# A four-layer graph network on one core: layer 1's norm from accumulated row sums and ScalarE squares

## The chip, the core and the metric

The kernel runs on one core of one Trainium2 chip. A core has TensorE (PE; its weight loads are listed as PEld), VectorE (DVE), ScalarE (ACT), GpSimd (POOL) and SyncE (SP, which here only starts DMAs). The metric is the device time of one execution in microseconds.

## The reference

Sixteen graphs ("batches") of 1024 nodes with 256 features pass through four layers. Each layer normalises its input over the features, applies relu, runs a graph operation with the adjacency matrix, and adds the result to its input. Layers 0 and 1, where the change lies:

```python
# layernorm: (x - mean) / sqrt(var + 1e-5), over the last axis
h = jnp.maximum(_layernorm(x), 0.0)
x = x + L0(h, adj)        # attention-like weights: a = u / sum(u), u = mask * exp(e + f)
h = jnp.maximum(_layernorm(x), 0.0)
x = x + L1(h, adj)        # d^-1/2 adj d^-1/2 @ (h @ weight) + bias
```

Layer 2 is a recurrence over the nodes, layer 3 a product with the adjacency matrix and a two-layer network. Both read what layers 0 and 1 have left in DRAM.

## The kernel before

A batch's x is held in SBUF as 8 tiles of 128 nodes x 256 features. `layers_0_1` fixes the order of the instructions of all five engines by hand: each engine runs its queue in program order, so an instruction that waits holds up everything behind it on that engine.

For each batch i the loop does an "a half" (layer 0) and a "d half" (layer 1). Each half forms its product with the adjacency matrix in `sums`, as seven block products on quarters of the matrix (`b11`, `b21`, `t1` to `t4`, `b22`), into the PSUM banks px, py and pz. The sums and differences of quarters (`add_halves`, L620) and of activations (`combos`: `s1`, `s2`, then two more) are made by VectorE. Between the block products the code calls hooks (`a0` to `a6`, `d0` to `d6`), which put other work into the engines' queues: loads, the next batch's statistics, and `side(...)`, which gives VectorE pieces of the ordering work that layer 2 needs.

After the a half, `weights` multiplies the result by layer 0's matrix `w0`: TensorE makes two tiles at a time into one of three `pmm` buffers (L418), and VectorE adds each tile, scaled, to x (L421). Layer 1's norm needs the mean and variance of these new rows. Before the change the `then` argument calls `stats` after each tile, so VectorE runs bn_stats (L323) and bn_aggr (L324) for it. Then `inv_sqrt` lets VectorE scale and POOL raise to the power -1/2 (L82, L86), VectorE forms `rd` and `shift` (L712, L714), and ScalarE's `normed` writes relu((x - mean) * scale) into `h1` (L353), which the first product of the d half reads. While that goes on, TensorE runs the product with `w1` of the *previous* batch (`second_weights`: two pairs before, two pairs behind the place where `run_a.turn` stands). Batch 0 has no previous batch.

The *next* batch's statistics for layer 0 are made by ScalarE, in the class `Moments`: `first` sums the rows (L337), `middle` lets VectorE form the negative mean (L340), `second` sums the squares of x minus the mean (L345), `root` makes the power. Their unneeded elementwise output goes to a scrap tile of PSUM, named `pt`, of which there are two buffers. `second(lo)` for the first four tiles stands in hook `a6`, `second(hi)` for the other four between `sums` and `weights`.

From batch 9 on the loop also prepares two batches per turn for layer 2, as `Job`s. `run_a.turn()` transposes a batch on TensorE into the same two `pt` buffers, in four groups (L535), and ScalarE copies each group out (L538); `run_a.rest()` (`first`, `order`, `base`) follows after the second `w1` pairs, and ends with stores issued by POOL. Batches 14 and 15 are prepared after the loop, where x[15] also gets its `w1` product and its norm.

At the very start VectorE copies the vector `v` out of PSUM (L603), a product of TensorE (L309) that needs loaded weights, then makes the statistics of batch 0 (`stats`), then the sums `add_f` (L437) that lead over `end_f` (L443) to the products of `degrees` (L459).

Of the kernel before, what the change touches and what calls it, by code (L numbers as in the profile page):

```python
# [9 lines left out]
F32 = mybir.dt.float32  # L10
AF = mybir.ActivationFunctionType
ALU = mybir.AluOpType
# [4 lines left out]
P = 128  # L17
B, N, D, H = 16, 1024, 256, 1024
NT = N // P
# [12 lines left out]
LN_EPS = 1e-5  # L32
# [4 lines left out]
def bcast_row(ap, n):  # L37

    return bass.AP(tensor=ap.tensor, offset=ap.offset, ap=[[0, P], [1, n]])
# [3 lines left out]
def gnn_stack(ctx: ExitStack, tc: tile.TileContext, a: dict, out: bass.AP):  # L43
    nc = tc.nc
# [30 lines left out]
    def rows(ap):  # L75
        return ap.rearrange("(t p) d -> p t d", p=P)

    def inv_sqrt(pool, src, eps, shape, name, mul=1.0):

        t = pool.tile(shape, F32, name=name + "_v")  # L80
        if mul == 1.0:
            nc.vector.tensor_scalar(t, src, eps, None, op0=ALU.add)  # L82
        else:
            nc.vector.tensor_scalar(t, src, mul, eps, op0=ALU.mult, op1=ALU.add)
        r = pool.tile(shape, F32, name=name)
        nc.gpsimd.tensor_tensor(r, t, mhalf.to_broadcast(shape), ALU.pow)  # L86
# [177 lines left out]
    def layers_0_1():  # L264
        with ExitStack() as st:
# [54 lines left out]
            def stats(x, tiles, mv):  # L320
                for t in tiles:
                    s6 = small.tile([P, 6], F32, name="s6", bufs=4)
                    nc.vector.bn_stats(s6, x[:, t])  # L323
                    nc.vector.bn_aggr(mv[:, t], s6)  # L324

            class Moments:


                def __init__(self, x):
                    self.x = x  # L330
                    self.ssq, self.neg = (small.tile([P, NT], F32, name=n) for n in ("m_ssq", "m_neg"))
                    self.sum = small.tile([P, NT], F32, name="m_sum", bufs=1)

                def first(self, tiles):
                    junk = psum.tile([P, 512], F32, name="pt")[:, :D]
# [4 lines left out]
                    nc.vector.tensor_scalar(self.neg, self.sum, -1.0 / D, None, op0=ALU.mult)  # L340

                def second(self, tiles):
                    junk = psum.tile([P, 512], F32, name="pt")[:, :D]
                    for t in tiles:
                        nc.scalar.activation(junk, self.x[:, t], AF.Square, bias=self.neg[:, t : t + 1],  # L345
                                             accum_out=self.ssq[:, t : t + 1])

                def root(self):
                    self.rs = inv_sqrt(small, self.ssq, LN_EPS, [P, NT], "rs", mul=1.0 / D)

            def normed(h, x, shift, scale, tiles):
                for t in tiles:
                    nc.scalar.activation(h[:, t], x[:, t], AF.Relu, bias=shift[:, t : t + 1], scale=scale[:, t : t + 1])  # L353
# [56 lines left out]
                hooks[6]()  # L410
                return ag

            def weights(x, ag, w, scale, then=lambda t: None, pairs=range(0, NT, 2)):
                for t0 in pairs:
                    po = psum.tile([P, 2, D], F32, name="pmm", bufs=3)
                    for t in (t0, t0 + 1):
                        for c in range(DC):
                            nc.tensor.matmul(po[:, t - t0], ag[:, c, t * P : (t + 1) * P], w[:, c],  # L418
                                             start=c == 0, stop=c == DC - 1)
                    for t in (t0, t0 + 1):  # L420
                        nc.vector.scalar_tensor_tensor(x[:, t], po[:, t - t0], scale[:, t : t + 1], x[:, t],  # L421
                                                       op0=ALU.mult, op1=ALU.add)
                        then(t)

            def begin_f(b, tiles):
                m = mean[b]
# [173 lines left out]
            all_ = range(NT)  # L600
            lo, hi = range(NT // 2), range(NT // 2, NT)

            nc.vector.tensor_copy(v, pv)  # L603
            mean[0] = m = Moments(x[0])
            mv = small.tile([P, NT, 2], F32, name="mv")
            stats(x[0], all_, mv)
            m.neg = small.tile([P, NT], F32, name="m_neg")
            nc.vector.tensor_scalar(m.neg, mv[:, :, 0], -1.0, None, op0=ALU.mult)
            m.rs = inv_sqrt(small, mv[:, :, 1], LN_EPS, [P, NT], "rs")
            nc.sync.dma_start(vec["W_b"], bcast_row(a["W_b"], D))  # L610
            nc.sync.dma_start(w0, a["W_wT"].rearrange("(c p) e -> p c e", p=P))
            begin_f(0, all_)
# [26 lines left out]
            for i in range(B):  # L639
                run_a, run_b = jobs.get(i, (None, None))  # L640
                here, ahead, behind = i < B, i + 1 < B, i > 0
                got = {}
# [7 lines left out]
                def a1():  # L650
                    if ahead:
                        get(i + 1, "b11", 0, 0)
                    second()
                    add_halves(i, "t4", "t2", "b21")
# [50 lines left out]
                pairs = list(range(0, NT, 2))  # L705
                second_weights(pairs[:2])
                pairs = pairs[2:]
                if run_a:
                    run_a.turn()
                if here:  # L710
                    rd = small.tile([P, NT], F32, name="rd")
                    nc.vector.tensor_mul(rd, rs, dis[i])  # L712
                    shift = small.tile([P, NT], F32, name="shift")
                    nc.vector.scalar_tensor_tensor(shift, mv[:, :, 0], -1.0, rd, op0=ALU.mult, op1=ALU.mult)  # L714
                    h1[i] = big.tile([P, NT, D], F32, name="h1")
                    normed(h1[i], x[i], shift, rd, all_)
                    if ahead:
                        mean[i + 1].root()
# [10 lines left out]
                m2 = Moments(x[i - 1]) if behind else None  # L729
# [80 lines left out]
            mv = small.tile([P, NT, 2], F32, name="mv")  # L810
# [6 lines left out]
            nc.vector.scalar_tensor_tensor(shift, mv[:, :, 0], -1.0, rs, op0=ALU.mult, op1=ALU.mult)  # L817
# [5 lines left out]
            normed(h2[15], x[15], shift, rs, all_)  # L823
            nc.sync.dma_start(rows(he_d[15]), h2[15])
            job15.load()
            job14.first()
# [596 lines left out]
    def layer_3(shared, x, hn, at, h, eye):  # L1423
        with ExitStack() as st:
# [274 lines left out]
            for b in range(B):  # L1699
# [91 lines left out]
```

## Time and profile before

| what | value |
|---|---|
| median of 3 runs | 4239.55 us (4235.62 to 4241.14) |
| the profiled execution | 4237.46 us, span in the profile 4235.8 us |
| busy, share of the span | PE 95%, DVE 63%, POOL 39%, ACT 37% |
| layers 0 and 1 | about the first 1340 us of the span |
| DMA, mean over the span | 176 GB/s |

The profile is one execution on the chip. For each engine it gives the instructions with start and duration, and for each idle stretch the instruction that ended it (written `<-`). A row of a timeline holds the start in us, the duration or, for merged rows, the stretch in us, the engine, the line of the kernel, the operation, the output and the inputs, and in brackets the idle time before it with its releaser. A matmul in f32 appears as two instructions. The granted TensorE clock is given as a share of full speed.

### The profile page before, as it was taken

How to read it: one execution, taken by the hardware profiler on the slowest of the kernel's cores; microseconds unless marked ns; L12 is line 12 of the kernel's file. 1: busy time of each engine (PE TensorE's matmuls, PEld its weight loads, DVE VectorE, ACT ScalarE, POOL GpSimd, SP SyncE). 2: the span in 40 equal slices, each digit the busy share in tenths (PEclk: the TensorE clock that was granted, in tenths of full speed). 3: DMA queues.
4: the chain of work that ended last, by engine and by line, in shares of the span. 5: the costliest groups of instructions: out<-in, count | busy, mean ns of one | idle time of the engine just before them, and what ended most of it. 6: DMA issues, size and time to landing. Idle time of an engine off the chain costs nothing. (4 is left out here: it accounts for less than half of the span.)

```text
span 4235.8 us, 56395 instructions
## 1 busy us (share of the span) xinstructions
PE 4031.0 (95%) x19307; PEld 2803.9 (66%) x19307; DVE 2676.5 (63%) x6286; ACT 1552.3 (37%) x3900; POOL 1644.6 (39%) x1740
## 2 busy tenths in 40 slices
PE   7999999999997999999999999998899999999998
PEld 3545455555555888888888888877365665756656
DVE  7889887478873445444444444453577777777776
ACT  3454545444433232322323232323333334333332
POOL 2132323443434323243333333332546355464552
PEclk9999999999998999999999999998899999999999
DMA  6667666988858454646454645431533434434320
GB/s 234 213 219 238 201 216 232 282 283 290 307 190 267 142 180 155 194 136 200 136 190 148 195 155 180 140 113 36 206 127 130 169 118 142 139 120 171 118 100 20
DMA packets 406701, 744.72 MB, mean 176 GB/s; under 512 B 75168, under 2 KB 325664, under 8 KB 365344
## 3 DMA queue, kind: packets, MB, share of 16 engines
q1 hardware_dynamic: 370976, 613.49, 42.3%
q0 software_dynamic: 26080, 109.21, 9.1%
q10 hardware_dynamic: 9216, 16.78, 1.1%
q8 instruction: 210, 3.44, 0.3%
q14 instruction: 219, 1.79, 0.1%
HBM read 538.85 MB, written 183.76 MB: 171 GB/s over the span
## 5 line engine op out<-in xcount | busy, mean ns | idle before, releaser
L86 POOL TENSOR_TENSOR rs<-rs_v,mhalf 128x8 f32<-128x8 f32 (+1 forms) x65 | 112.2, 1727 | 931.8 <-DVE rs_v L82 720.5
L928 PE MATMUL pf<-hb,ab 128*128 128x256 f32 x1568 | 415.2, 383 | 0.0
L1041 PE MATMUL pf<-hs,wx 128*128 128x256 f32 x1536 | 348.0, 383 | 11.6 <-POOL hs L1032 11.4
L1041 PEld LDWEIGHTS pf<-hs,wx 128*128 128x128 f32 x1536 | 293.7, 192 | 55.0 <-POOL hs L1032 12.6
L1569 POOL TENSOR_TENSOR ss<-ss,sq 128x512 f32<-128x512 f32 x224 | 299.0, 1350 | 24.5 <-ACT sq L1567 18.5
L1341 POOL DMA_INDIRECT hs_d<-h,table x128 | 128.9, 1007 | 461.4 <-ACT gates L1049 401.7
L928 PEld LDWEIGHTS pf<-hb,ab 128*128 128x128 f32 x1568 | 272.1, 191 | 37.3 <-issue 6.7
L1046 DVE TENSOR_TENSOR gates<-pf,bias 128x512 f32<-128x512 f32 x128 | 88.4, 691 | 285.3 <-PE pf L1041 285.2
L418 PE MATMUL pmm<-w,ag 128*128 128x256 f32 x1024 | 242.6, 391 | 27.0 <-DVE x L421 13.8
L1632 PEld LDWEIGHTS po<-w,hh 128*128 128x128 f32 x2048 | 238.2, 193 | 16.6 <-issue 11.0
L418 PEld LDWEIGHTS pmm<-w,ag 128*128 128x128 f32 x1024 | 194.8, 194 | 77.2 <-DVE x L421 31.2
L1632 PE MATMUL po<-w,hh 128*128 128x128 f32 x2048 | 242.4, 277 | 1.4 <-ACT hh L1615 0.7
L1567 ACT ACTIVATE sq<-hh 128x512 f32<-128x512 f32 x224 | 141.2, 630 | 198.0 <-POOL ss L1569 113.8
L1515 PE MATMUL ph<-bxt,hb 128*128 128x512 f32 x440 | 199.5, 599 | 3.3 <-ACT hb L1487 1.9
L1139 ACT ACTIVATE r<-pr 128x128 f32<-128x128 f32 (+2 forms) x256 | 57.8, 278 | 361.6 <-PE pr L1095 356.6
L1077 PE MATMUL pf<-bd,h 128*128 128x384 f32 (+4 forms) x512 | 184.6, 450 | 0.8 <-DVE bxt L1080 0.8
L1080 DVE TENSOR_TENSOR bxt<-bxt,pf 128x384 f32<-128x384 f32 (+4 forms) x256 | 127.7, 500 | 82.0 <-PE pf L1077 79.6
L1565 DVE SCALAR_TENSOR_TENSOR hh<-ph,b,u 128x512 f32<-128x512 f32 x192 | 141.2, 749 | 47.2 <-PE ph L1561 37.4
L1615 ACT ACTIVATE hh<-hh,rw 128x512 f32<-128x512 f32 x256 | 158.7, 709 | 23.7 <-DVE hh L1614 23.7
L1614 DVE TENSOR_TENSOR hh<-hh,po 128x512 f32<-128x512 f32 x256 | 154.3, 673 | 2.9 <-PE po L1611 2.9
L345 ACT ACTIVATE pt<-x,m_neg 128x256 f32<-128x256 f32 x240 | 114.3, 476 | 107.8 <-DVE m_neg L340 101.5
L1515 PEld LDWEIGHTS ph<-bxt,hb 128*128 128x128 f32 x440 | 82.8, 192 | 101.2 <-issue 93.7
(363 smaller groups left out, 9225.9 us busy)
## 6 DMA issues: line engine op xcount, KB each, us to landing
at<-in_quarters SPq DMA_DIRECT2D x94, 1024.0 KB, 9.9
t_d<-at SPq DMA_DIRECT2D x64, 1024.0 KB, 11.5
ab<-in_columns SPq DMA_DIRECT2D x127, 512.0 KB, 5.0
bxt<-t_d SPq DMA_DIRECT2D x42, 1024.0 KB, 4.8
bxt<-in_quarters SPq DMA_DIRECT2D x34, 1024.0 KB, 4.8
at<-at POOLq DMA_DIRECT2D x30, 1024.0 KB, 10.8
at<-t_d SPq DMA_DIRECT2D x22, 1024.0 KB, 6.2
pc<-in_own ACTq DMA_DIRECT2D x64, 256.0 KB, 7.2
```

What stands on the lines that cost most here:

```text
L418: nc.tensor.matmul(po[:, t - t0], ag[:, c, t * P : (t + 1) * P], w[:, c], start=c == 0, stop=c == DC - 1)
L928: nc.tensor.matmul(pb, ab[:, jts[k]], hb[:, jts[k]], start=k == 0, stop=k == len(jts) - 1)
L1041: nc.tensor.matmul(pg[:, e], wx[:, c, q * D + e * P : q * D + (e + 1) * P], self.hs[:, c], start=c == 0, stop=c == DC - 1)
L1077: nc.tensor.matmul(pf, h[:, g, c * P : (c + 1) * P], bd[:, g, b0 : b0 + n, S : S + far], start=True, stop=True)
L1341: nc.gpsimd.indirect_dma_start(out=hs_d[t][g][:, :], out_offset=row(1, g, t, s), in_=h[:, g], in_offset=None)
L1515: nc.tensor.matmul(pa, st[left][:, k], at[q % 6][:, k], start=onto is None and k == 0, stop=k == 3, skip_group_check=True)
L1565: behind3[:] = [nc.vector.scalar_tensor_tensor(hh[q][:, k], ph, b1[:, k : k + 1], u, op0=ALU.add, op1=ALU.add)]
L1567: nc.scalar.activation(sq, hh[q][:, k], AF.Square)
L1569: nc.gpsimd.tensor_tensor(ss[q], ss[q], sq, ALU.add)
L1614: nc.vector.tensor_mul(hh[q][:, k], hh[q][:, k], pr)
L1615: nc.scalar.activation(hh[q][:, k], hh[q][:, k], AF.Silu, scale=rw[:, k : k + 1])
L1632: nc.tensor.matmul(po[:, n], left[:, c, n * P : (n + 1) * P], right[:, c], start=onto is None and n == 0 and c == 0, stop=c == HH - 1, ski ...
```

## The change

`weights` no longer calls `stats`. With `norm` given, each of VectorE's additions also delivers the sum of the new row (`accum_out`). After each pair of tiles `pair` lets VectorE form the two negative means and puts two squares with accumulation into ScalarE's queue; their elementwise output goes to the first tile of `h1`, which is allocated earlier for this. `root` then makes the power. The next batch's `second(hi)` now comes after `weights` and `root`. The same is done for x[15] after the loop, with `s2` as scrap. At the start, v's copy moves behind the statistics of batch 0.

```diff
+                def pair(self, t):
+                    two = slice(t, t + 2)
+                    nc.vector.tensor_scalar(self.neg[:, two], self.sum[:, two], -1.0 / D, None, op0=ALU.mult)
+                    self.second((t, t + 1))
...
-            def weights(x, ag, w, scale, then=lambda t: None, pairs=range(0, NT, 2)):
+            def weights(x, ag, w, scale, norm=None, pairs=range(0, NT, 2)):
...
+                        more = {"accum_out": norm.sum[:, t : t + 1]} if norm else {}
                         nc.vector.scalar_tensor_tensor(x[:, t], po[:, t - t0], scale[:, t : t + 1], x[:, t],
-                                                       op0=ALU.mult, op1=ALU.add)
-                        then(t)
+                                                       op0=ALU.mult, op1=ALU.add, **more)
+                    if norm:
+                        norm.pair(t0)
...
-            nc.vector.tensor_copy(v, pv)
             mean[0] = m = Moments(x[0])
...
             m.rs = inv_sqrt(small, mv[:, :, 1], LN_EPS, [P, NT], "rs")
+            nc.vector.tensor_copy(v, pv)
...
-                    mv = small.tile([P, NT, 2], F32, name="mv")
+                    h1[i] = big.tile([P, NT, D], F32, name="h1")
+                    m1 = Moments(x[i], "n", h1[i][:, 0])
+                    weights(x[i], ag, w0, got["rc"], m1)
+                    m1.root()
                     if ahead:
                         mean[i + 1].second(hi)
-                    weights(x[i], ag, w0, got["rc"], lambda t: stats(x[i], (t,), mv))
-                    rs = inv_sqrt(small, mv[:, :, 1], LN_EPS, [P, NT], "rs")
...
-                    nc.vector.tensor_mul(rd, rs, dis[i])
+                    nc.vector.tensor_mul(rd, m1.rs, dis[i])
                     shift = small.tile([P, NT], F32, name="shift")
-                    nc.vector.scalar_tensor_tensor(shift, mv[:, :, 0], -1.0, rd, op0=ALU.mult, op1=ALU.mult)
-                    h1[i] = big.tile([P, NT, D], F32, name="h1")
+                    nc.vector.tensor_mul(shift, m1.neg, rd)
...
-            weights(x[15], ags[15], w1, dis[15], lambda t: stats(x[15], (t,), mv))
+            m2 = Moments(x[15], "n", big.tile([P, 2, D], F32, name="s2").rearrange("p a d -> p (a d)")[:, :D])
+            weights(x[15], ags[15], w1, dis[15], m2)
             nc.sync.dma_start(rows(x2_d[15]), x[15])
-            rs = inv_sqrt(small, mv[:, :, 1], LN_EPS, [P, NT], "rs")
+            m2.root()
```

More of the change, by code (lines that the diff above doesn't have):

```diff
@@ L326, in layers_0_1, with __init__ @@
             class Moments:
[L329 to L332, printed above, removed]
+                def __init__(self, x, name="m", junk=None):
+                    self.x, self.junk = x, junk
+                    self.ssq, self.neg = (small.tile([P, NT], F32, name=name + n) for n in ("_ssq", "_neg"))
+                    self.sum = small.tile([P, NT], F32, name=name + "_sum", bufs=1)
                 def first(self, tiles):
@@ L342, in second @@
                 def second(self, tiles):
-                    junk = psum.tile([P, 512], F32, name="pt")[:, :D]
+                    junk = self.junk if self.junk is not None else psum.tile([P, 512], F32, name="pt")[:, :D]
                     for t in tiles:
@@ L809, in layers_0_1 @@
             job14.load()
-            mv = small.tile([P, NT, 2], F32, name="mv")
-            weights(x[15], ags[15], w1, dis[15], lambda t: stats(x[15], (t,), mv))
+            m2 = Moments(x[15], "n", big.tile([P, 2, D], F32, name="s2").rearrange("p a d -> p (a d)")[:, :D])
+            weights(x[15], ags[15], w1, dis[15], m2)
             nc.sync.dma_start(rows(x2_d[15]), x[15])
-            rs = inv_sqrt(small, mv[:, :, 1], LN_EPS, [P, NT], "rs")
+            m2.root()
             run_b.first()
@@ L816, in layers_0_1 @@
             shift = small.tile([P, NT], F32, name="shift")
-            nc.vector.scalar_tensor_tensor(shift, mv[:, :, 0], -1.0, rs, op0=ALU.mult, op1=ALU.mult)
+            nc.vector.tensor_mul(shift, m2.neg, m2.rs)
             job14.mask()
@@ L822, in layers_0_1 @@
             h2[15] = big.tile([P, NT, D], F32, name="h2", bufs=2)
-            normed(h2[15], x[15], shift, rs, all_)
+            normed(h2[15], x[15], shift, m2.rs, all_)
             nc.sync.dma_start(rows(he_d[15]), h2[15])
```

## The prediction

> **What bounds the kernel now.** I read the page's engine totals first, then TensorE's waits in the first 1340 us (layers 0 and 1), then the timelines of one vector-bound batch and one batch with layer 2's preparation.
>
> ```profile
> PE 4031.0 (95%) x19307; PEld 2803.9 (66%) x19307; DVE 2676.5 (63%) x6286; ACT 1552.3 (37%) x3900; POOL 1644.6 (39%) x1740
> ```
>
> TensorE is busy for 95% of the span, so an edit on another engine pays only where TensorE waits. Its waits (total us, times, longest):
>
> ```profile
> PE pmm L418 <- DVE x L421: 13.8, 8, 2.9
> PE pt L459 <- ACT gs L443: 12.3, 1, 12.3
> ...
> PE pt L558 <- ACT hT L565: 8.2, 6, 4.0
> ...
> PE px L382 <- ACT h L353: 8.0, 1, 8.0
> ```
>
> The change touches three of these: the weight product waiting for the vector's additions (L418), the start (L459), and batch 0's wait for layer 1's norm (L382). Everything it can gain lies there. Batch 1, vector then TensorE:
>
> ```profile
> 131.89 0.48 DVE L421 SCALAR_TENSOR_TENSOR x<-pmm,rc,x 128x256 f32<-128x256 f32 x1
> 132.40 0.43 DVE L323 BATCH_NORM_STATS2 s<-x 128x6 f32<-128x256 f32 x1
> 132.86 0.18 DVE L324 BATCH_NORM_AGGREGATE mv<-s 128x2 f32<-128x6 f32 x1
> 132.96 0.45 DVE L421 SCALAR_TENSOR_TENSOR x<-pmm,rc,x 128x256 f32<-128x256 f32 x1
> ```
> ```profile
> 133.46 10.59 PE L418 MATMUL pmm<-w,ag 128*128 128x256 f32 x40 [2.04 <-DVE x L421]
> 143.89 3.60 PE L382 MATMUL px<-at,h 128*128 128x512 f32 x8
> ```
>
> A tile costs the vector 1.06 us (131.89 to 132.96), a pair 2.1, while TensorE makes a pair in 1.72 (13.7 us for eight, from batches that flow). With three pmm buffers TensorE falls to the vector's pace.
>
> Batch 11, where `turn` stands between the weight products, ScalarE and TensorE:
>
> ```profile
> 890.82 1.07 ACT L538 COPY hT<-pt 128x512 f32<-128x512 f32 x2 [6.26 <-issue]
> ```
> ```profile
> 890.14 1.04 PE L535 MATMUL pt<-to,h 128*128 128x128 f32 x8
> 891.46 1.15 PE L535 MATMUL pt<-to,h 128*128 128x128 f32 x8 [0.28 <-ACT hT L538]
> 892.44 3.62 PE L418 MATMUL pmm<-w,ag 128*128 128x256 f32 x16
> ```
>
> ScalarE had been idle for 6.26 us when the transposes came, so its copies followed at once. That idle time is what the change fills.
>
> [...] TensorE's waits of 3.48 us (batch 13), but also of 2.75, 2.08 and 2.04 us (batches 14, 12, 1) are followed by a granted 0.50; waits of 1.94, 2.84, 2.88 and 2.95 us are not. Batch 13's stage (busy time of PE, PEld, DVE, ACT and POOL, then the granted clock, DMA share, GB/s):
>
> ```profile
> 1070.00:1072.00 2.00, 2.00 (x5) 1.64 (x6) 1.82 (x9) 1.90 (x7) 0.00 (x0) 0.50 1.00 422
> ```
>
> [...] the trace shows no overtaking, and my loss rests on this. [...] The trace agrees, on L437, and gives the price:
>
> ```profile
> 511.49 0.48 DVE L437 SCALAR_TENSOR_TENSOR pt<-q,rs,v 128x256 f32<-128x256 f32 x1
> 511.89 0.14 DVE L437 DVE_READ_ACCUMULATOR pt<-q,rs,v 128x1 f32 x1
> 512.14 0.49 DVE L437 SCALAR_TENSOR_TENSOR pt<-q,rs,v 128x256 f32<-128x256 f32 x1
> ```
>
> **The change, part by part.** L421 with an accumulator is not in the trace; L437 has the same form and repeats every 0.655 us. `pair` adds a 128x2 scaling, about 0.08. So a pair costs the vector 1.39 us (bounds: 1.3 with the scaling hidden, 1.6 if the read waits for the write), against 2.1. ScalarE gets eight squares a batch at 0.632 each (L345's rhythm), 5.06 us, and in its queue they stand *ahead of* the second half of the next batch's squares (four, 2.53 us).
>
> Call the vector's first addition t0. Vector-bound, the last scaling starts at t0 + 5.5; ScalarE follows 0.2 later and ends its last two squares at t0 + 7.0, the next batch's half at H = t0 + 9.53. The vector stands still from 5.6 to 7.15 because `root` waits for ScalarE; behind it wait the four additions of the previous batch's w1 product, so TensorE's last pair starts at t0 + 8.15, just about when it would anyway. From rs_v to ScalarE's first `normed` the trace has 2.45 us (140.44 to 142.89), hence t0 + 9.6, and TensorE's px at t0 + 10.25.
>
> *Batches 1 to 8.* t0 is set by ordering work ahead of it, which stays. Batch 1: t0 = 131.89, px 142.14 against 143.89: 1.75. Batches 2 to 5: t0 + 11.66 now, so 1.4 each, 5.6. Batch 6 has only 0.67 us over its 13.7 to give: 0.65. Batches 7 and 8: 1.3 each. Sum 10.6; less 0.7 because batch 1's half clock (from 134.85) may now bind: **-9.9**.
>
> *Batch 0.* No w1 product fills the wait; px at t0 + 11.59 becomes t0 + 10.25: **-1.4**. TensorE still idles some 6.7 us, so the cold product behind it (5.94 us instead of 3.6) stays.
>
> *The start.* Statistics need only x. The SP queue's waits before its quarter loads place x's last pair at about 6.95 us; eight tiles at 0.525 then end at about 8.0, the power at 10.1, and v's copy (its product ends at 10.10) is done at 10.5. The sums of L437 start at 10.6 instead of 16.87, `degrees` at 16.1 instead of 22.39: 6.3 earlier. Quarters b11, b21 and t3 have landed by 12.21, 14.66 and 17.06 (what the SP queue waits for); b22, by that step, at 19.5, when it is needed. Late next is t1, due at about 22 by the same 2.4 us step: L620's additions, 22.46 before, start at 22.0. They were hidden; now their chain to s2 (10.26 us, 22.46 to 32.72) ends at 32.2, TensorE has waited since 28.1, and it starts that product at 32.3 instead of 34.44, half-clocked after a 4 us wait (about 2 us back). Bounds: nothing, and 4 us if t1 lands at 20.5 and the clock holds. I take **-1**.
>
> *Batches 9 to 14.* `turn` stands behind all those squares in ScalarE's queue. Its second transpose group needs the pt buffer that the next batch's last squares use as scrap, and its copies come behind them. So the group starts at H + 0.1 and the last pairs of w1 at H + 1.9 (copy 0.57, transposes 0.5, twice) = t0 + 11.4. Before it was t0 + 9.93 in batches 9, 11 and 13: +1.5 each. Batch 10 flows at TensorE's pace (H = 783.48 + 12.6): +1.8, of which about 1.4 counts, since `order` then waits for the heT_d store, which is issued later too. Batch 12 was late already: +0.6; batch 14, half-clocked through its w0 pairs: +1.7. With 1.58 for batch 9 the sum is **+8.3**; `order`, `first` and the d half follow unshortened. Batch 15 has no next batch: 0. The turn's wait (T(A) ends at t0 + 7.0, the next group starts at 9.6) is 2.6 us, in the length where four of eight throttled: three times 1.8 us, **+5.4** (bounds 0 and 11).
>
> *The end.* x[15]'s squares queue behind h2[14]'s norm (to 1310.6) and end at 1315.7; bs and run_b's copies behind them were at 1314.88. Everything to the last he_d store and job15's load follows: **+0.8**.
>
> What leaves the vector (8 x 0.4 us a batch) is worth nothing beyond this: its queue empties every batch at L366. SP and POOL issue the same instructions in the same order; the powers only move.
>
> Sum: -9.9 - 1.4 - 1 + 8.3 + 5.4 + 0.8 = **+2.2 us** on the profiled execution's 4237.46 (span 4235.8), which is 2.1 under the median of the three runs. On the median: 4241.8.
>
> **Rivals.** A measurement of this kernel tells about 0.2% (8.5 us) from no change: below 4231.1 and above 4248.0.
>
> *Cancel (0.58).* As summed, 4242. For it: gains and losses come out of the same queue. Against: its terms are each uncertain by a few us.
>
> *Slower (0.25).* One mechanism: the 2.6 us wait inside `turn` throttles TensorE every time. Six times 2 us instead of three times 1.8: +8.8, 4248.4. It decides from six throttled turns on, or five with the start giving nothing. For it: four of eight such waits did; against: three as long or longer didn't.
>
> *Faster (0.17).* The turn costs 0.6 as in batch 12 (3.6 in all), no wait throttles, and t1 lands early (start -4): -10.6 - 1.4 - 4 + 3.6 + 0.8 = -11.6, 4228. Against: the two pt buffers and the queue's order.
>
> *It doesn't do what it says:* `normed` isn't earlier in batches 1 to 8, because the next batch's squares ahead of it end later than the power does. At 9.53 against 9.6 it is a tie; each 0.3 us more per batch moves the sum by 2.4. It is inside the range.
>
> **How the numbers follow.** 4242, the cancelling case; the range 4231 to 4253 leaves out about 1 in 10 on each side and reaches both rivals' edges.
>
> **What would show it.** Right: L421 with its accumulator read at a 0.65 us rhythm; waits of L418 on L421 falling to what is left of t0; px 1.3 to 1.8 us earlier behind t0 in batches 1 to 8; the second transpose group of `turn` waiting on ScalarE for 2 to 3 us in batches 9 to 14; the clock row showing 0.5 after some of them; L620 waiting for a quarter at 22 us. Wrong: turns as short as before (2.3 us), or the first s2 product before 30 us.

## The result, and the profile after

| | time, us | against before |
|---|---|---|
| before | 4241.14 median of 17 runs (4233.61 to 4246.18) | |
| after | 4228.27 median of 17 runs (4219.63 to 4235.39) | 0.9972, 95% interval 0.9966 to 0.9978 |
| after, profiled execution | 4226.12, span 4224.4 (before: 4237.46, span 4235.8) | |

The change makes the kernel 12.9 us faster (0.28%), where 4242 was predicted, with a range of 4231 to 4253. Line numbers move: L421 of before is L427 now, L418 is L423, L382 is L387, L353 is L358, L535/L538 are L542/L545, L437 is L444, and L350 is the new scaling of a pair; in the experiments' kernels lines behind an edit are one to ten higher. L153 to L158 and L216 to L226 belong to the ordering work, which the change does not touch. First the engine totals of the page of after:

```profile
PE 4018.3 (95%) x19307; PEld 2802.1 (66%) x19307; DVE 2614.6 (62%) x6218; ACT 1635.4 (39%) x4172; POOL 1646.5 (39%) x1740
```

The vector gave up 62 us and ScalarE took 83; neither decides. What decides is TensorE's waits in layers 0 and 1 (after; total us, times, longest):

```profile
PE pt L542 <- ACT pt L345: 10.5, 6, 2.2
PE pmm L423 <- DVE x L427: 8.8, 7, 1.9
...
PE pt L466 <- ACT gs L450: 6.1, 1, 6.1
PE px L387 <- ACT h L358: 6.1, 1, 6.1
...
PE pt L225 <- DVE o_key L226: 2.9, 1, 2.9
```

The waits of the weight product for the vector fell by 5.0 us, the start's by 6.2, batch 0's by 1.9. `turn` has the new wait that the prediction described: on ScalarE's squares, six times, up to 2.2 us. The ordering work's wait, L225, fell from 5.9 to 2.9, which the prediction did not have; the second profiles show below that the change has no part in that.

Batch 1 of after on the vector, whose first addition is t0 = 127.67:

```profile
127.67 0.48 DVE L427 SCALAR_TENSOR_TENSOR x<-pmm,rc,x 128x256 f32<-128x256 f32 x1
128.07 0.08 DVE L427 DVE_READ_ACCUMULATOR x<-pmm,rc,x 128x1 f32 x1
128.07 0.48 DVE L427 SCALAR_TENSOR_TENSOR x<-pmm,rc,x 128x256 f32<-128x256 f32 x1
128.48 0.08 DVE L427 DVE_READ_ACCUMULATOR x<-pmm,rc,x 128x1 f32 x1
128.59 0.17 DVE L350 TENSOR_SCALAR n_neg<-n_sum 128x2 f32<-128x2 f32 x1
128.67 0.48 DVE L427 SCALAR_TENSOR_TENSOR x<-pmm,rc,x 128x256 f32<-128x256 f32 x1
```

The second addition starts 0.40 us after the first: the accumulator's read (0.08) is done while it starts. A pair costs 1.00 us (127.67 to 128.67), not 1.39. On ScalarE the eight squares then run back to back, two in about 1.32 us, from 128.86 to 134.06 (t0 + 6.4), the next batch's four to 136.46, and the norm starts at 136.48 (t0 + 8.8). ScalarE, the last square of each kind and the norm (rows between left out), then TensorE in the same stretch:

```profile
133.46 0.51 ACT L345 ACTIVATE h<-x,n_neg 128x256 f32<-128x256 f32 x1
...
135.86 0.48 ACT L345 ACTIVATE pt<-x,m_neg 128x256 f32<-128x256 f32 x1
...
136.48 4.05 ACT L358 ACTIVATE h<-x,shift,rd 128x256 f32<-128x256 f32 x8
```

```profile
128.62 8.90 PE L423 MATMUL pmm<-w,ag 128*128 128x256 f32 x40 [1.41 <-DVE x L427]
137.35 3.60 PE L387 MATMUL px<-at,h 128*128 128x512 f32 x8
```

40 matmuls in 8.90 us is TensorE's own pace: the granted clock is 1.00 here (from 68 to 792 us) and no wait stands between them. px follows without a gap at t0 + 9.68.

Where the time went, by stage, in us against the first profile of before (negative: earlier), taken from the starts of the same TensorE instructions. "after again" and "before again" are second profiles of the same kernels, from the experiments; the last column is the mean of the two after less the mean of the two before.

| stage | predicted | after | after again | before again | mean difference |
|---|---|---|---|---|---|
| start, to batch 0's w0 product | -1 | -2.70 | -0.70 | +2.75 | -3.1 |
| batch 0, to batch 1's w0 product | -1.4 | -1.53 | -1.57 | +0.46 | -1.8 |
| batches 1 to 8 | -9.9 | -14.52 | -14.73 | +0.23 | -14.7 |
| batches 9 to 14, to px of 14 | +13.7 | +9.17 | +6.37 | +0.73 | +7.4 |
| ordering work, batch 15, x[15], to layer 2 | +0.8 | -6.06 | -3.86 | -3.39 | -3.3 |
| layers 2 and 3 | 0 | +4.30 | +0.98 | +3.84 | +0.7 |
| end | +2.2 | -11.34 | -13.51 | +4.62 | -14.7 |

The last column adds to -14.7 against 12.9 on the medians: single executions of one kernel differ by up to 3.8 us in a stage (layers 2 and 3 of before). Batches 1 to 8 repeat to 0.3 us in these four profiles, which all have full clock behind a wait of 2.95 us in batch 7; three versions below that have the same code up to there have half clock behind it and gain only 12.9 to 13.0. The stages from batch 9 on do not repeat, and are read with that in mind.

Batch 11 of after, ScalarE and TensorE (here t0 = 864.52):

```profile
872.70 0.48 ACT L345 ACTIVATE pt<-x,m_neg 128x256 f32<-128x256 f32 x1
873.21 0.57 ACT L545 COPY hT<-pt 128x512 f32<-128x512 f32 x1
```
```profile
870.75 0.60 PE L542 MATMUL pt<-to,h 128*128 128x128 f32 x4
873.36 2.44 PE L542 MATMUL pt<-to,h 128*128 128x128 f32 x12 [2.00 <-ACT pt L345]
875.60 4.48 PE L423 MATMUL pmm<-w,ag 128*128 128x256 f32 x16
```

The last of the next batch's squares is followed at once by `turn`'s first copy: TensorE had one group done at 871.3 and waited 2.0 us. 16 matmuls take 4.48 us here and 3.62 at full clock: the granted clock was 0.50 from 873.92 to 877.33 us.

### The profile page after: what moved, and what is told of

It is laid out like the page before. It is cut to its first block, busy times and chain, and to the rows that moved or that the text cites. A ratio compares the mean times of both kernels' runs of the same rounds, so it can differ in the third digit from the quotient of the medians.

```text
span 4224.4 us, 56649 instructions
## 1 busy us (share of the span) xinstructions
PE 4018.3 (95%) x19307; PEld 2802.1 (66%) x19307; DVE 2614.6 (62%) x6218; ACT 1635.4 (39%) x4172; POOL 1646.5 (39%) x1740
## 5 line engine op out<-in xcount | busy, mean ns | idle before, releaser
L423 PE MATMUL pmm<-w,ag 128*128 128x256 f32 x1024 | 234.6, 387 | 20.4 <-DVE x L427 8.8
L423 PEld LDWEIGHTS pmm<-w,ag 128*128 128x128 f32 x1024 | 196.1, 194 | 61.6 <-DVE x L427 12.6
L1494 ACT ACTIVATE hb<-x,shift,rs 128x256 f32<-128x256 f32 x120 | 60.9, 591 | 239.6 <-DVE shift L1492 239.6
```

## The experiments

Theory: the mechanisms of the prediction are the right ones (gain where the vector held the weight product, loss where `turn` stands behind squares in ScalarE's queue), but the price of a pair was too high and the loss in `turn` too large. Rivals are named with each group. In the tables px is TensorE's first product of the d half.

### What a pair may cost

One scrap operation of the vector ahead of each pair's scaling, or two of them, in batches 0 to 15:

```diff
                     if norm:
+                        nc.vector.scalar_tensor_tensor(norm.pad, x[:, t0], 1.0, x[:, t0], op0=ALU.mult, op1=ALU.add)
                         norm.pair(t0)
```

> The kernel after with one more 128x256 scalar_tensor_tensor on the vector (0.41 us, its result is scrap) ahead of each pair's scaling in layer 1's norm, so that a pair costs the vector 1.4 us, which is what the prediction reckoned, instead of the 1.0 us that the trace of after shows. Theory A (the pair's price is the term that was too large): the last scaling comes 1.6 us later, the last squares end near t0 + 7.0 instead of t0 + 6.4, and px starts 0.6 us later behind t0 in batches 1 to 5, about 3 us over batches 1 to 8: about 0.998 of before. Rival (ScalarE's eight squares at 0.63 us set the norm, whatever a pair costs the vector): px as in after within 0.2 us, 0.9972.

> The kernel after with two more 128x256 scalar_tensor_tensor (results are scrap) ahead of each pair's scaling. One of them made a pair 1.21 us instead of 1.0 and moved the norm's start from t0 + 8.8 to t0 + 9.0, but px stayed at t0 + 9.68, where TensorE ends the w1 product in its own pace. Theory A (norm and TensorE's own pace were within 0.05 us of each other; from there on the pair's price counts in full): a pair now costs 1.5 to 1.6 us, the last two squares end at t0 + 7.4 to 7.7, the norm starts at t0 + 9.9 to 10.2, px at t0 + 10.5 to 10.9: each of batches 1 to 5 gains 0.9 to 1.2 us less than after. Rival (TensorE's products alone set px, the norm has room): px stays at t0 + 9.7 in batches 1 to 5.

| | pair, us | norm starts | px | gain of batches 1 to 5 at px | time |
|---|---|---|---|---|---|
| after | 1.00 | t0 + 8.8 | t0 + 9.68 | 10.6 | 0.9972 |
| padded | 1.21 | t0 + 9.0 | t0 + 9.68 | 10.2 | 0.9973 (0.9962 to 0.9984), 4225.5 |
| padded twice | 1.55 | t0 + 10.1 | t0 + 10.72 | 4.8 | 4250.2, one run; before beside it 4237.6 |

The first pad moved the norm by 0.2 and px by nothing: the expectation of 0.6 us fell, because the pad made a pair 1.21 and not 1.4, and because px stood where TensorE's own products end. Padded, TensorE:

```profile
131.19 8.90 PE L423 MATMUL pmm<-w,ag 128*128 128x256 f32 x40 [1.42 <-DVE x L427]
139.92 3.67 PE L387 MATMUL px<-at,h 128*128 128x512 f32 x8
```

The rival, that ScalarE's squares set the norm, is half right: as long as a pair costs the vector less than ScalarE's 1.32 us for its two squares, ScalarE sets the norm. The second pad goes beyond that: padded twice, ScalarE waits 0.32 to 0.34 us for the vector ahead of each of the last three pairs. Padded twice, vector (batch 1, t0 = 132.14), then TensorE:

```profile
132.95 0.76 DVE L432 SCALAR_TENSOR_TENSOR ds<-x 128x256 f32<-128x256 f32 x2
133.62 0.16 DVE L350 TENSOR_SCALAR n_neg<-n_sum 128x2 f32<-128x2 f32 x1
133.69 0.48 DVE L427 SCALAR_TENSOR_TENSOR x<-pmm,rc,x 128x256 f32<-128x256 f32 x1
```
```profile
133.09 7.17 PE L423 MATMUL pmm<-w,ag 128*128 128x256 f32 x32 [1.41 <-DVE x L427]
140.83 1.99 PE L423 MATMUL pmm<-w,ag 128*128 128x256 f32 x8 [0.56 <-DVE x L427]
142.86 3.70 PE L387 MATMUL px<-at,h 128*128 128x512 f32 x8
```

The eight matmuls at the end now wait for the vector's w1 additions, which stand behind `root`'s wait for ScalarE, and px waits for the norm. With 0.55 us more on each pair the same change costs 12.6 us in its one run instead of gaining 13: batches 1 to 8 gain 3.5 instead of 14.5 (1.7 of that difference is the half clock in batch 7, which this profile has), and batches 9 to 14 lose 15.9. There the waits inside `turn` are 3.3 us in four batches and 1.7 in two, as what stands ahead of it in ScalarE's queue ends later. 4.3 us of the 12.6 fall into layers 2 and 3, which the pads don't touch, but at layer 2's start the kernel was already 8 us behind the first profile of before. So the price of a pair decides the sign, and the prediction's 1.39 lies between.

### What an accumulator read costs

The products with v (L444) were the row that the prediction priced the new additions by. Their scrap goes to SBUF, and then to four places in turn:

```diff
-                    nc.vector.scalar_tensor_tensor(junk, q[b][:, t], m.rs[:, t : t + 1], v[:, :D],
+                    out = m.ds[:, :D]                            # accum_sbuf
+                    out = m.ds[:, t % 4 * D : t % 4 * D + D]     # accum_alternate
+                    nc.vector.scalar_tensor_tensor(out, q[b][:, t], m.rs[:, t : t + 1], v[:, :D],
```

> The kernel after, but the products with v (scalar_tensor_tensor with an accumulator, 0.655 us from one to the next, scrap in PSUM) write their scrap into ds's tile in SBUF. Theory A (an accumulator read costs 0.24 us more where the operation writes PSUM): the rhythm falls to 0.41 us, as with layer 0's additions in after, and the read to 0.08 us. Rival (the place of the result does not matter; two operands from SBUF, or the broadcast-free v, make it slow): it stays at 0.65 us. Time: what is saved, 2 us a batch, lies where TensorE waits for little; 0 to 5 us faster than after, 0.996 to 0.997 of before.

> accum_sbuf with one more change: the scrap of the products with v goes in turn to four slices of ds's tile instead of always to the same one. In accum_sbuf the rhythm fell only from 0.655 to 0.595 us. Theory A (an operation that writes where the one before it wrote waits for that one's end): 0.41 us, as with layer 0's additions, each of which writes another tile of x. Rival (the scale taken from rs and the operand v, both from SBUF, or the wait itself cost it): it stays at 0.59 us. Time: as accum_sbuf, 0.9965 of before, 0 to 2 us faster.

The vector at the start of accum_sbuf, then of accum_alternate:

```profile
10.81 0.48 DVE L445 SCALAR_TENSOR_TENSOR ds<-q,rs,v 128x256 f32<-128x256 f32 x1
11.22 0.08 DVE L445 DVE_READ_ACCUMULATOR ds<-q,rs,v 128x1 f32 x1
11.41 0.48 DVE L445 SCALAR_TENSOR_TENSOR ds<-q,rs,v 128x256 f32<-128x256 f32 x1
```
```profile
11.53 0.48 DVE L445 SCALAR_TENSOR_TENSOR ds<-q,rs,v 128x256 f32<-128x256 f32 x1
11.94 0.08 DVE L445 DVE_READ_ACCUMULATOR ds<-q,rs,v 128x1 f32 x1
11.94 0.48 DVE L445 SCALAR_TENSOR_TENSOR ds<-q,rs,v 128x256 f32<-128x256 f32 x1
```

The rhythm goes from 0.655 to 0.60 when the scrap leaves PSUM, and to 0.41 when two operations in a row no longer write the same place. Of the 0.245 us between the ends, the shared scrap is 0.185, three quarters, and PSUM 0.06. The instruction records of the traces, which the timeline leaves out where they only wait, show what holds the second operation back: with a shared scrap a semaphore wait of the program stands between the two, on the semaphore that the accumulator's read before it raises (accum_sbuf: read until 11.31, wait until 11.37, next operation at 11.41). accum_alternate has no such wait ahead of its second and third operation, nor have layer 0's additions within a pair. So it is an ordering that the program asks for, and before's rows at L437 have it too (read until 17.42, wait until 17.48, next operation at 17.52). The times, 0.9969 (0.9956 to 0.9982) and 0.9965 (0.9951 to 0.9978), cannot be told from after's 0.9972: up to 2 us a batch taken from the vector buys nothing measurable.

### Where turn's wait comes from

turn_first puts the next batch's last squares behind `turn`, norm and order in batches 9 to 14; turn_scrap leaves every queue as it is and takes only the pt buffer away from the squares; norm_0_to_8 gives batches 9 to 15 the old statistics; old_queue puts the four squares back ahead of the weight product in all batches.

```diff
                     m1.root()
-                    if ahead:
+                    if ahead and not run_a:                  # turn_first
                         mean[i + 1].second(hi)
...
                     run_a.rest()
+                    if ahead:                                # turn_first; root() follows in hook d1
+                        mean[i + 1].second(hi)
```
```diff
                     if ahead:
+                        if run_a:                            # turn_scrap
+                            mean[i + 1].junk = h1[i][:, 1]
                         mean[i + 1].second(hi)
```

```diff
+                    if not run_a:                            # norm_0_to_8
                         m1 = Moments(x[i], "n", h1[i][:, 0])
                         weights(x[i], ag, w0, got["rc"], m1)
                         m1.root()
                     if ahead:
                         mean[i + 1].second(hi)
+                    if run_a:
+                        weights(x[i], ag, w0, got["rc"], then=lambda t: stats(x[i], (t,), mv))
+                        rs = inv_sqrt(small, mv[:, :, 1], LN_EPS, [P, NT], "rs")
```
```diff
+                    if ahead:                                # old_queue
+                        mean[i + 1].second(hi)
                     weights(x[i], ag, w0, got["rc"], m1)
                     m1.root()
-                    if ahead:
-                        mean[i + 1].second(hi)
```

> The kernel after, but in batches 9 to 14 the last four squares of the next batch's statistics and their power stand behind turn, norm and the order's copies in ScalarE's and the vector's queues (the power in the d half) instead of ahead of turn. Theory A (place in ScalarE's queue): the six waits of turn's second transpose group, 10.5 us in after, fall to about 0.3 us each where the weight product's own squares are done by then, to under 1 us in the others, and no half clock follows them; with the cost of the turns gone, 8 to 9 us faster than after, 0.995 of before. Rival 1 (what delays turn is this batch's own eight squares, not the next batch's four): the waits stay at 1 us or more and the gain is under 3 us. Rival 2: the four squares are missed later, the d half waits for the power (add_f on rs) or px's copies, and half of the gain is given back.

> The kernel after, but in batches 9 to 14 the next batch's last four squares write their scrap into h1's tile and not into a pt buffer; the order of every queue stays. Theory A (place in ScalarE's queue): turn's second group transposes at once, the wait goes to the third group, which needs ScalarE's copy of the first, and is only some 0.5 us a batch shorter: 2 to 4 us faster than after, 0.9965 of before. Rival (the pt buffer is what is missing): turn's waits end, 8 to 9 us faster than after, 0.995.

> The kernel after, but batches 9 to 14, which hold a turn, and batch 15 take layer 1's statistics as in the kernel before (BN_STATS on the vector, the next batch's last squares ahead of the weight product); batches 0 to 8, the start and x[15] stay as after. Theory A: the loss of 8.8 us that the trace of after shows from batch 9 to batch 14 comes from what this takes out, so TensorE is some 18 us ahead of before at batch 14's px (after: 9.6) and the program 8 to 9 us faster than after, about 0.995 of before. Rival 1: the loss comes from elsewhere (the earlier batches run into a transfer that keeps its own time, once they are ahead by 18 us), and batches 9 to 14 lose it here too: as after, 0.9972. Also open: the 3.9 us that after gains at the ordering work's transposes (L225's wait on L226). If relief of the vector in batches 9 to 15 gives them, they are gone here and one operation in front of them is 4 us or longer, as before; if it is chance who comes first, the vector or GpSimd's additions, it may stay or go, whatever the vector was spared.

> The kernel after, but the next batch's last four squares stand ahead of the weight product in every batch, as in the kernel before. Theory A (ScalarE's queue is what both the gain and the loss hang on): in batches 1 to 5 ScalarE is idle for only 1.1 us ahead of the first of layer 1's squares and the four take 2.5, so norm and px come 1.4 us later, some 7 us less gain; in batches 9 to 14 turn is let go 1 to 2.5 us earlier, some 4 to 9 us less loss; together within 4 us of after, 0.996 to 0.998. Rival (the place of these four squares makes no difference in batches 1 to 8, since they end anyway when the norm could start, 136.46 against 136.45 us in batch 1): px in batches 1 to 5 as in after and only the turns gain, 4 to 9 us faster than after, about 0.9955.

| | turn's waits in batches 9 to 14, us | batches 9 to 14 | batches 1 to 5 at px | time |
|---|---|---|---|---|
| after, two profiles | 2.2, 1.2, 2.0, 2.0, 2.0 or 1.1, 1.1 or 2.5 | +9.2, +6.4 | 10.6 | 0.9972 |
| turn_scrap | 2.2, 1.2, 2.0, 2.0, 1.9, 1.2 (third group) | +5.1 | as after | 0.9964 (0.9951 to 0.9978) |
| old_queue | 2.2, 1.2, 0.4, 0.2, 0.2, 0.8 | +0.3 | 4.3 | 0.9979 (0.9969 to 0.9989) |
| norm_0_to_8 | 0.3 each | +1.0 | as after | 0.9952 (0.9939 to 0.9966) |
| turn_first | 0.2 each | +1.1 | as after | 0.9945 (0.9932 to 0.9959) |

Batch 11 on TensorE, turn_scrap, then turn_first:

```profile
871.01 1.04 PE L542 MATMUL pt<-to,h 128*128 128x128 f32 x8
874.07 1.43 PE L542 MATMUL pt<-to,h 128*128 128x128 f32 x8 [2.02 <-ACT hT L545]
```
```profile
874.41 1.04 PE L542 MATMUL pt<-to,h 128*128 128x128 f32 x8
875.68 1.15 PE L542 MATMUL pt<-to,h 128*128 128x128 f32 x8 [0.24 <-ACT hT L545]
```

With a free buffer two groups are transposed instead of one, and the wait is as long as before (2.02 us in batch 11, 2.00 in after), for the copy: the place in ScalarE's queue is the cause. The buffer adds one group, some 0.5 us by the trace; that the stage's +5.1 is less than after's is no more than what profiles differ by. Out of the queue, the wait is gone and with it the stage's loss; turn_first and norm_0_to_8 are then as before again (+0.7) in these batches, within what profiles differ. That the four squares would be missed later has only this for it: TensorE's waits for L407 and for order's copies add to 17.5 us instead of 12.5, and the stage total is none the worse.

old_queue shows that the same four squares, ahead of the weight product, take 6.3 us of the gain in batches 1 to 5: the change needs them behind the weight product there, and behind `turn` later.

### The start

```diff
-            nc.vector.tensor_copy(v, pv)
             mean[0] = m = Moments(x[0])
...
+            nc.vector.tensor_copy(v, pv)
             nc.sync.dma_start(vec["W_b"], bcast_row(a["W_b"], D))
```

> The kernel before with one edit: the copy of v behind batch 0's statistics. Theory A (the trace of after read stage by stage): the first s2 product starts at 31.7 us instead of 34.44, because quarter t1 has landed by 21.3 us, and its 2.5 us wait does not halve the clock; all that follows in layers 0 and 1 is 2.7 us earlier, so 0.9994 of before. Rival (the prediction's sizing): t1 lands at 22, the wait halves the clock, 1 us, 0.9998. Second rival: the earlier start is lost again where batch 0 or 1 waits for something with a time of its own, and batch 1's weight product starts no earlier than 125.88 us.

start_only (before with v's copy behind the statistics) gave 0.9988 (0.9981 to 0.9994), 4233.5 us. In its profile batch 1's weight product starts 2.1 us earlier than in before, so the start's gain isn't lost on the way, as the second rival has it. After's start, on the vector and on TensorE:

```profile
21.28 7.84 DVE L627 TENSOR_TENSOR at<-at,at 128x1024 f32<-128x1024 f32 x4 [4.76 <-DMA at<-in_quarters]
```
```profile
31.66 3.67 PE L387 MATMUL px<-at,s 128*128 128x512 f32 x8 [2.52 <-DVE s L372]
```

after_v_first is the other way round, after with v's copy in its old place:

```diff
+            nc.vector.tensor_copy(v, pv)
             mean[0] = m = Moments(x[0])
...
-            nc.vector.tensor_copy(v, pv)
             nc.sync.dma_start(vec["W_b"], bcast_row(a["W_b"], D))
```

> The kernel after with v's copy again ahead of batch 0's statistics. Theory A (the start's share of the gain is small and changes from execution to execution: it was 0.6 to 3.4 us at batch 0's weight product in ten profiles, with two at zero): the start is as in before, 0 to 3 us slower than after, 0.997 to 0.998 of before. Rival (start_only's 0.9988 is the start's whole share, 5 us): 5 us slower than after, 0.9983. The ordering work's instruction at L216 takes 1.35 us, if 4.90 us does not come from the place of v's copy.

It gave 0.9977 (0.9967 to 0.9986), 4229.4 us, and +1.07 us at batch 0's w0 product. All profiles with v's copy behind lie between -3.4 and +0.9 us there (thirteen, mean -1.3), the three with it ahead between 0 and +2.8 (mean +1.3). The move is worth about 2.6 us; start_only's median shows 5, with an interval from 2.5 to 8, and after_v_first against after some 2. The s2 product's wait for the vector, 2.5 us in after, lasted from 1.5 to 4.3 us in these thirteen profiles: the additions on quarter t1 start between 20.6 and 22.4 us, and TensorE comes to the product between 26.8 and 31.2. Half clock begins within 1.5 us of the product's start in eight of the thirteen, where its eight matmuls take 5.30 to 6.55 us, and not in after's, where they take 3.67.

start_only also shows what else moves a single execution. Its TensorE in batch 7, then that of turn_first_sbuf (below), with the same wait:

```profile
551.19 0.30 PE L158 MATMUL pt<-ident,o_pos 128*128 128x128 f32 x1 [2.96 <-DVE o_pos L155]
551.33 5.30 PE L382 MATMUL pz<-at,q 128*128 128x512 f32 x8
```
```profile
538.84 0.30 PE L158 MATMUL pt<-ident,o_pos 128*128 128x128 f32 x1 [2.95 <-DVE o_pos L155]
538.97 3.60 PE L387 MATMUL pz<-at,q 128*128 128x512 f32 x8
```

Every kernel here has this wait of 2.95 or 2.96 us. After it the eight matmuls took 3.60 us in six profiles and 4.9 to 5.3 in ten.

### Second profiles

> The kernel before, unchanged, for a second profiled execution. In the first one a vector instruction of the ordering work (L216, 0.29 us elsewhere) took 4.90 us at 1222.49 us, and TensorE waited 5.9 us at L225; in all thirteen other profiles it took 1.35 us. If that is chance, it takes 1.35 us here and TensorE waits 2.9 us. If it belongs to this kernel's timing, it takes some 4.9 us again.

> The kernel after, unchanged, for a second profiled execution and for times beside the other versions. 0.9972 of before. If the half clocks after turn's waits are a matter of the kernel, batches 11, 12 and 13 show them again; if they are a matter of the moment, other turns do. The ordering work's wait at L225 is 2.9 us again, if the 5.92 us of before were the exception.

Both kernels unchanged. after_again: 0.9971 (0.9960 to 0.9982), 4224.0 us. Half clocks follow turn's waits in batches 11 and 12, not 13, where the wait is 1.1 us this time (in after: 11, 12 and 13, each with 2.0 us). before_again: 4242.1 us, and the operation at L216 took 1.35 us, TensorE's wait at L225 2.4. So before's 5.9 us there belong to that one execution. What held the vector (before, vector and GpSimd):

```profile
1222.49 4.90 DVE L216 SCALAR_TENSOR_TENSOR o_junk<-o_sub,o_bins 128x128 f32<-128x128 f32 x1
```
```profile
1222.92 0.59 POOL L578 DMA_DIRECT2D base_d<-bo  x1
1223.54 3.70 POOL L357 TENSOR_TENSOR x<-x,W_b_sb 128x512 f32<-128x512 f32 x3
```

The operation ends at 1227.39, when GpSimd's three additions do (1227.24); most of the fifteen operations of its line take 0.29 us. In the other fifteen profiles it takes 1.35 us and ends just behind GpSimd's last DMA issue (in after at 1214.08, the issue at 1213.98), when the additions have just begun (1214.00). An earlier one of the line ends in the same way behind three other additions (in before at 1190.00, the additions at 1189.84), after 3.7 us, in thirteen of the sixteen profiles, all but those with turn_first's edit. No run moved GpSimd's additions; that they hold the vector is read from these ends.

### A version that is faster

turn_first_sbuf and turn_first_alternate add the two scrap edits to turn_first.

> turn_first with accum_sbuf's edit: the next batch's last squares behind turn, norm and order in batches 9 to 14, and the scrap of the products with v in SBUF. If the two act in different stages they add up: turn_first's 0.9945 of before and 0 to 4 us more, 0.9935 to 0.9945. Rival: in the d half the late power meets the shortened products with v, which wait for it, and it is no faster than turn_first.

> turn_first with accum_alternate's edit. What is saved on the vector by accum_alternate (0.24 us eight times a batch, if its theory holds) lies ahead of a wait of TensorE's (pz on L407, 5.6 us in nine) and behind others that hide it: 0 to 4 us faster than turn_first, 0.9935 to 0.9947 of before, and 10 to 13 us faster than after_again. Rival: it is hidden, as turn_first, 0.9945 to 0.995.

They gave 0.9950 (0.9936 to 0.9963) and 0.9952 (0.9939 to 0.9966): the rival's answer, as turn_first alone, for nothing measurable. turn_first alone, at 0.9945 (4216.5 us), has the lowest time against before of all versions; its interval and after's do not meet, but it can't be told from norm_0_to_8 or from these two.

## Why the prediction was wrong, step by step

The forecast was +2.2 us on the profiled execution, and the last column of the stage table has -14.7. Of these 16.9 us, 6.3 lie in batches 9 to 14, 4.8 in batches 1 to 8, 4.1 behind batch 14 and 2.1 at the start. Of the 4.1, before's first profile accounts for 1.8 and the rest is open. Two steps failed: the price of a pair, and the half clock that was added for `turn`.

**The pair's price (batches 1 to 8, -9.9 predicted, -14.5 to -14.7 measured).** The step that failed is "so a pair costs the vector 1.39 us", with bounds of 1.3 and 1.6: it is 1.00. The row it was taken from, L437, has the same form, but writes one scrap in PSUM again and again, with the program's wait in between, and layer 0's additions each write their own tile. From there the sum followed: squares ended at t0 + 6.4 instead of 7.0, H came at 8.8 instead of 9.53, px at 9.68 instead of 10.25. That is 0.57 us in each of batches 1 to 5, 2.9 in all, most of the 3.2 missing there: from their w0 products to batch 6's they gained 9.8, where 1.75 + 5.6 - 0.7 = 6.65 was reckoned. Batches 6 to 8 gained 4.7 instead of 3.25; why was not followed further. Batch 1's half clock, reckoned at 0.7, did not come; its wait had fallen from 2.04 to 1.41 us.

**The tie.** "At 9.53 against 9.6 it is a tie" was the right place to look: norm and next batch's squares do meet (136.48 against 136.46), and 0.34 us more on a pair (padded twice against padded) cost 5.4 us over five batches. It was put down as a reason to fear a later norm, and not as a reason to ask what L437's 0.655 us consists of.

**The turn (+8.3 for the delay and +5.4 for half clock predicted, +9.2 and +6.4 measured in two profiles, delay and clock together).** The mechanism was right and is shown: the second group waits on ScalarE, 2.0 us in batch 11, because of the queue. In batch 11 it starts at t0 + 8.84 (9.63 predicted), the last pairs at t0 + 11.08 (11.4). What failed is the second term, "three times 1.8 us, +5.4". The 1.8 us is near what before's trace shows: behind the wait of 2.08 us in batch 12, 24 matmuls took 7.13 us with the granted clock at 0.50 for 3.41 us of it, where the pace of 16 in 3.62 us gives 5.4. Three of six waits were followed by half clock, as predicted, but the stage has no more half clock than without the change. By the traces' record of the granted clock, TensorE has half clock for 17.1 us between 660 and 1185 us in before, in after and in turn_first, and for 20.5 us in both second profiles. Before has it for 6.8 us in batch 10 and behind L418's waits for the vector in 12, 13 and 14. After has it for 3.4 us in batch 10, behind `turn`'s waits in 11, 12 and 13 and behind the weight product's wait in 14. Some came as others went, and the net term is about zero.

The prediction took the half clock from the length of the wait, and the length alone does not decide it: of the sixteen waits of 2.95 or 2.96 us in batch 7 ten have half clock behind them and six have none. In the first profiles of before and after all stretches of half clock, 17 in each, start whole multiples of 3.41 us apart, and but for the last one in a profile last 3.41 us or a multiple of it. What decides which wait is followed by one was not shown.

**The start (-1) and batch 0 (-1.4).** Both right in mechanism and sign. t1's additions start at 21.28 instead of 22.0 and the product at 31.66 instead of 32.3. The half clock behind that product, reckoned at 2 us, did not come in after and came in eight of thirteen profiles; over the profiles the start is worth 2.6, inside the stated bounds of 0 and 4. Batch 0 measured -1.5 to -1.6.

**The end (+0.8).** Not seen: from batch 14's px to layer 2 after_again gains 3.9 and before_again 3.4 against the same first profile of before, so the two differ by 0.5 and not by the 6.1 that after's first profile shows.

**"What leaves the vector is worth nothing beyond this".** Held, as far as the times can tell: the two scrap edits take more from the vector and buy nothing measurable. The gain at L225 looks like an exception and is none. The first profile of before was unlucky there by 3.6 us against its second, so the first traces of before and after show a gain that the kernels don't have.

**The rivals.** The "faster" rival's 4228 is the measured number, by other terms: it counted on cheap turns and a start of 4 us; in fact the turns cost 6 to 9 and the batches without one gave 14.5. "Slower" needed half clock after every turn wait; the two profiles of after show two and three of six, and nothing added by them. The change does become slower than before, by another way: with a pair at 1.55 us.

## What to carry to other kernels

Price a new instruction from a row that agrees in what it writes as well as in its form: the rhythm of operations that share a scrap contains the wait for it (0.60 us here, 0.41 with a place for each). Where two engines' chains arrive within 0.1 us of each other, work out from which price on the answer changes sign, and measure that price first. When work moves to an engine with idle time, follow what was using the idle time: here moving four squares of the next batch behind the copies that TensorE needs made the same change worth nearly twice as much (0.55% against 0.28%).

## What the runs showed of the hardware

- A 128x256 scalar_tensor_tensor with an accumulator repeats every 0.41 us when each writes its own place in SBUF (accum_alternate, and layer 0's additions in after). It repeats every 0.60 us when all write one place in SBUF and every 0.655 when all write one place in PSUM, in both cases with a semaphore wait of the program between two operations. The accumulator's read takes 0.08 us with a result in SBUF and 0.14 in PSUM.
- Stretches of half clock (granted 0.50) start on a grid of 3.41 us in the first profiles of before and after, 17 stretches in each. The same wait of TensorE, 2.95 or 2.96 us in the same place, is followed by half clock in ten of sixteen executions, for 1.3 to 1.7 us each. Waits of 2.0 us in `turn` were followed by it too (batches 11, 12 and 13 of after), and the longer one of 2.2 us in batch 9 of after was not.
- Two vector operations that were under way while GpSimd's additions ran ended with them or up to 0.6 us later: one at L216 of before took 4.90 instead of 1.35 us and ended 0.15 us behind three additions, one at L153 in batch 7 of before took 6.10 instead of 0.68 us and ended 0.55 us behind four additions of 5.23 in all. By their records both start 0.3 to 1.1 us before the first addition, beside a DMA issue of GpSimd; why they were held was not shown. In fifteen of sixteen profiles the operation at L216 took 1.35 us, 3.6 less.
- ScalarE and VectorE took up their work in the order of their queues. In batch 11 of after `turn`'s first copy starts at 873.21, behind the square of 872.70, though TensorE had the group done at 871.3. In batch 1 of after the vector stood still for 2.27 us, until the squares let `root`'s first step start at 134.09, and the four w1 additions behind it came at 134.17.
- The stretch of layers 2 and 3, whose instructions are the same in all these kernels, differed by up to 4.3 us between the four profiles of before and after.
